# A bidirectional state-space layer with a soft mixture of experts: the order of the first transfers, of the constants and of the first silu

## The chip, the core and the metric

The kernel runs on one core of one Trainium2 chip. The metric is the device time of one launch in microseconds (us), from executions on the chip; the kernel before has a median of 5432.52 us over 3 runs (5432.14 to 5433.58). A core has five engines with a queue of instructions each: PE (matmul), DVE (vector), ACT (activation functions), POOL (a second vector engine) and SP, which here only issues DMAs. Each engine takes its instructions in the order of its queue; an instruction that waits for a semaphore holds everything behind it on that engine.

## What is computed

Sixteen sequences of 512 positions and 256 channels pass two layers, each with a residual and a layer norm. Cut to what matters:

```python
xr = x @ in_proj_w.T                      # 256 -> 2 x 512
xf, res = split(xr)
xf = silu(causal_conv(xf, conv_w, conv_b))          # 4 taps over positions
y  = ssm(xf, res, x_proj_w, dt_proj_w, dt_proj_b, A_log, D)
xb = silu(causal_conv(xf, conv_b_w, conv_b_b))
y += ssm(xb, res, ..., reverse=True)
x  = layernorm(x + y @ out_proj_w.T)
# ssm: A = -exp(A_log); dt, B, C = x @ x_proj_w.T; dt = softplus(dt @ dt_proj_w.T + b)
#      per state n of 16: a scan over the positions with decay exp(dt*A), input dt*u*B, output times C
#      y = (sum over states + u * D) * silu(res)

# second layer, a soft mixture of 16 experts with 64 slots each
x  = layernorm(x) * g + b
se = layernorm(slot_embeds) * slot_g + slot_b, times scale
logits = x @ se.T ; dispatch = softmax over positions ; combine = softmax over slots
slots = dispatch.T @ x ; eout = (gelu(slots @ Wg + bg) * (slots @ Wu + bu)) @ Wd + bd
x  = layernorm(x + combine @ eout)
```

## The kernel before

One sequence is handled at a time, channels on the 128 partitions and positions along the free axis. The 512 inner channels are four chunks (`ND`). For each sequence `scan_part` runs four times (forward and backward scan, two pairs of chunks); it walks over the 16 states in twos. For each pair of states and chunk POOL multiplies the input (`db`), ACT makes the decay (`h`, an exponential) and a factor (`th`, a tanh), DVE scans (`h`) and scales (`hg`), POOL multiplies by C (`hg` by `cs`), and PE adds the result up by transposing it into a PSUM bank (`acc`). The inputs `bs` and `cs` are broadcast rows of B and C, read back from a small DRAM buffer `bc`, which SP fills from `xd`.

Beside these scans the kernel does the rest in pieces. Generators yield after a group of matmuls; `beside_scan` takes one piece at a time from three lists: `prep` (the next chunks: `prep_forward`, `turn_back`, `prep_backward`, `prep_gate`, `prep_pair`), `front` (`moe_setup`, then `finish` of each sequence: output projection, layer norm, dispatch), and `back` (`experts` and `combine`, from sequence 3 on in every second sequence). The layer norms of these pieces go through `row_moments` (DVE: `bn_stats` and `bn_aggr` for each group of 128 rows), `factors` (POOL: the reciprocal root and the shift) and `scaled` (ACT).

Two things set the order of the instructions on each engine. The program text is the first. But a list scheduler stands behind it: it keeps the data dependences and moves instructions ahead of others where it expects their engine to be free. An instruction handed to `late` (`tc.keep_in_program_order`) keeps its place in the program's order relative to the others that are so marked; the unmarked ones may be put ahead of their place in the text. In `row_moments` of the kernel before nothing is marked, so the statistics of a group of rows can be put in as soon as these rows are there.

The beginning of the program is what most of the diff touches. In the kernel before it runs in this order:

- DVE clears `zeros` and `blank`; ACT issues four DMAs that clear `diag_dram` from `blank`.
- For the two directions in turn (the loop over `s, m`), SP loads the conv taps `cw`, `cb`, the three parts of `xT` (x_proj), `dtT`, `A`, `D`; ACT and DVE turn `A` into `-exp(A_log)` and half of it, and DVE fills the diagonal matrices `diagD`. Then SP loads `outT` (512 KB), which DVE halves.
- `prep_forward(0, 0, ND, fwd)` loads `x` of the first sequence with `load_x` (512 KB), PE transposes it (`ptx`), ACT copies it (`xT`); then for each chunk `project` loads 128 KB of `in_projT` (`w_pin`, two buffers), PE multiplies (`pin`), and `taps` forms the convolution: an Identity with scale and bias on ACT, then three multiply-adds on DVE. After the four chunks one silu covers all of them.
- `project_unit(0, 0, fwd)` multiplies by x_proj (`px`, four chunks accumulated in one bank), ACT evicts it (`xd`), SP writes `bc`, and ACT issues one DMA into `diag_dram`.
- `prep_pair(0, 0, 0, fwd)` makes the first two chunks of dt (`pz` on PE, softplus on ACT), `rr` (a scan on DVE) and `du` (POOL); then the first `scan_part` begins. `moe_setup`, whose tiles are the slot embeddings `se`, is listed first in `front`.

Each DMA of SP and ACT signals one of eight semaphores, taken in turn; a DMA that comes to a semaphore in use waits, in its queue, until the earlier DMA on it has landed.

Of the kernel before, what the change touches and what calls it, by code (L numbers as in the profile page):

```python
# [9 lines left out]
F32 = mybir.dt.float32  # L10
BF16 = mybir.dt.bfloat16
AF = mybir.ActivationFunctionType
# [5 lines left out]
P = 128  # L18
L = 512
NL = L // P  # L20
# [21 lines left out]

def row_moments(nc, pool, src, tag):

    k = src.shape[1]
    st = pool.tile([P, k, 6], F32, tag=f"{tag}_st", name=f"{tag}_st")
    mv = pool.tile([P, k, 2], F32, tag=f"{tag}_mv", name=f"{tag}_mv")
    for i in range(k):
        nc.vector.bn_stats(st[:, i, :], src[:, i, :])
        nc.vector.bn_aggr(mv[:, i, :], st[:, i, :])  # L50
    return mv


def seq_layers(tc, ident, neghalf, a, out):
# [22 lines left out]
    with ExitStack() as ctx:  # L77
# [33 lines left out]
        def load_x(b):  # L111
            xt = p1.tile([P, NL, DM], F32, tag="x", name=f"x_{b}")
            nc.sync.dma_start(xt, a["x"][b].rearrange("(c p) d -> p c d", p=P))
            return xt


        outT = const.tile([P, ND, DM], F32, name="outT")
        zeros = const.tile([P, L], BF16, name="zeros")
        nc.vector.memset(zeros, 0.0)
        blank = p2.tile([P, 4 * DM], F32, tag="W", name="blank", bufs=3)  # L120
        nc.vector.memset(blank, 0.0)
        for part in diag_dram.rearrange("r i l (p s) -> (r i) p l s", p=P):
            nc.scalar.dma_start(part, blank[:, : NL * (P + 1)].rearrange("p (l s) -> p l s", l=NL))

# [7 lines left out]

        side = []
        for s, m in (("f", ""), ("b", "_b")):
            w = {}
            w["cw"] = const.tile([P, ND, KW], F32, name=f"cw_{s}")
# [8 lines left out]

            nc.vector.tensor_scalar(w["xT"][:, :, XC:XW], w["xT"][:, :, XC:XW], 0.5, None, ALU.mult)
            w["dtT"] = const.tile([DTR + 1, DI], F32, name=f"dtT_{s}")
# [3 lines left out]
            nc.sync.dma_start(w["A"], a[f"A{m}_log"].rearrange("(c p) n -> p c n", p=P))  # L151
            nc.scalar.activation(w["A"], w["A"], AF.Exp)
            nc.vector.tensor_scalar(w["A"], w["A"], -1.0, None, ALU.mult)
            w["Ah"] = const.tile([P, ND, NS], F32, name=f"Ah_{s}")
            nc.vector.tensor_scalar(w["Ah"], w["A"], 0.5, None, ALU.mult)
            d = channels(a[f"D{m}"], f"D_{s}")
            w["diagD"] = const.tile([P, ND, P], F32, name=f"diagD_{s}")
            for c in range(ND):
                nc.vector.tensor_scalar(w["diagD"][:, c, :], ident, d[:, c : c + 1], None, ALU.mult)
            side.append(w)  # L160
        nc.sync.dma_start(outT, a["out_projT"].rearrange("(c p) o -> p c o", p=P))
        nc.vector.tensor_scalar(outT, outT, 0.5, None, ALU.mult)

        def late(ins):

            return tc.keep_in_program_order(ins)

# [15 lines left out]
        def project(xT, e, name, turned=False):  # L183

            wt = p2.tile([P, NM, P], F32, tag="inw", name=f"w_{name}")
            nc.sync.dma_start(wt, a["in_projT"].rearrange("(k p) e -> p k e", p=P)[:, :, e * P : (e + 1) * P])
            pp = bank(name)
            for lc in range(NL if turned else 0):
                s = slice(lc * P, (lc + 1) * P)
                for k in range(NM):  # L190
                    nc.tensor.matmul(pp[:, s], xT[:, k, s], wt[:, k, :], start=(k == 0), stop=(k == NM - 1))
            for k in range(0 if turned else NM):
                nc.tensor.matmul(pp, wt[:, k, :], xT[:, k, :], start=(k == 0), stop=(k == NM - 1))
            return pp

        def prep_forward(b, lo, hi, out):

            if lo == 0:
                xt = load_x(b)
                out["xT"] = p1.tile([P, NM, L], F32, tag="xT", name=f"xT_{b}")  # L200
# [11 lines left out]
            for c in range(lo, hi):  # L212
                yield GAP + 1
                pp = project(xT, c, f"pin_{b}_{c}")
                yield HOLD
                taps(xf[:, c, :], pp, side[0], c, xf[:, c, :])
            if hi == ND:
                yield 0
                late(nc.scalar.activation(xf, xf, AF.Silu))
                yield WAIT  # L220
                yield from project_unit(b, 0, out)
# [307 lines left out]
        def moe_setup():  # L529
# [4 lines left out]
            for t in (sg, sb):  # L534
                nc.vector.tensor_scalar(t, t, scale, None, ALU.mult)
            ses, src = [], a["slot_embeds"].rearrange("e s d -> (e s) d").rearrange("(h c p) d -> h p c d", p=P, c=4)
# [5 lines left out]
            yield 0  # L542
            stats = [factors(row_moments(nc, p2, se, "m1"), "m1") for se in ses]
            yield 0
# [44 lines left out]
        def finish(b, y):  # L589

            xt = load_x(b)
            for h in range(NL // 2):
# [25 lines left out]
                late(nc.vector.tensor_tensor(x2, x2, po, ALU.add))  # L618
            mv = row_moments(nc, p2, xt, "m1")
            yield WAIT  # L620
# [283 lines left out]
        def combine(b, kept=None):  # L904
# [20 lines left out]
            def moments(lo, hi):  # L925
                return row_moments(nc, p2, x1[:, lo:hi, :], f"c{hi - lo}"), f"c{hi - lo}"

# [140 lines left out]
```

## Time and profile before

| what | us |
|---|---|
| median of 3 runs | 5432.52 |
| the profiled execution, its own time | 5434.84 |
| the profiled execution, span of its instructions | 5432.9 |
| busy: POOL | 4732.3 |
| busy: DVE | 4552.0 |
| busy: PE | 4336.3 |
| busy: ACT | 4091.6 |
| POOL's first product (`du`) begins | 48.03 |
| first `db` of sequence 0, 1, 2, 3, 4, 5 begins | 50.7, 344.3, 643.3, 943.0, 1266.2, 1577.9 |
| first `db` of sequence 8, 9, 10 begins | 2548.5, 2857.8, 3184.6 |
| POOL idle within sequence 0, 1, 2 | 6.9, 5.8, 6.7 |
| POOL idle within sequence 8, 9 | 15.9, 30.6 |

The profile is of one execution; times inside it are counted from the start of its span, and its own time is 1.9 us longer than that span. A sequence here lasts from its first `db` on POOL to that of the next one. The last some 360 us, after the scans, are the tail: experts and combines of the last sequences, without POOL's products.

### The profile page before, as it was taken

What the parts mean: (1) busy time and instruction counts of PE and PEld (TensorE: products, weight loads), DVE (VectorE), ACT (ScalarE), POOL (GpSimd) and SP (SyncE); (2) the same over time, 40 slices, a digit from 0 to 9 for tenths busy, and PEclk for the clock granted to TensorE, in tenths of its full rate; (3) what the DMA queues carried; (4) which work ended last, traced back from release to release, by engine and by line L of the source; (5) the groups of instructions that cost most, each with busy time, mean ns of one, the idle gap of its engine ahead of it and who ended that gap; (6) DMA issues with size and microseconds to landing.
All of it is one profiled execution on the core that took longest, in us unless ns stands there. A gap on an engine that the chain in (4) does not pass through costs nothing. (4 is left out here: it accounts for less than half of the span.)

```text
span 5432.9 us, 73685 instructions
## 1 busy us (share of the span) xinstructions
PE 4336.3 (80%) x24145; PEld 3393.4 (62%) x24145; DVE 4552.0 (84%) x6276; ACT 4091.6 (75%) x6517; POOL 4732.3 (87%) x2537
## 2 busy tenths in 40 slices
PE   4656666898878977788788978889777887878889
PEld 3545555676667765677656766667656775667657
DVE  6888989889888898888988988988989889887722
ACT  6677777887788777887878887788778887777641
POOL 6999999999999899998999989998999989988600
PEclk7677878898889989899889988899888998989999
DMA  4333434575446754566446754467444774457435
GB/s 129 130 122 132 130 124 131 192 231 161 151 141 212 228 148 145 157 220 213 134 137 195 230 173 150 130 215 231 151 145 143 226 224 132 144 178 234 126 104 184
DMA packets 595237, 907.73 MB, mean 167 GB/s; under 512 B 78083, under 2 KB 384899, under 8 KB 594853
## 3 DMA queue, kind: packets, MB, share of 16 engines
q1 hardware_dynamic: 521156, 859.87, 49.9%
q10 hardware_dynamic: 73696, 43.14, 2.8%
q8 instruction: 192, 3.15, 0.2%
q14 instruction: 193, 1.57, 0.1%
HBM read 840.86 MB, written 62.01 MB: 166 GB/s over the span
## 5 line engine op out<-in xcount | busy, mean ns | idle before, releaser
L432 POOL TENSOR_TENSOR hg<-hg,cs 128x1024 f32<-128x1024 f32 x1024 | 2415.3, 2362 | 129.7 <-DVE hg L431 111.4
L403 POOL TENSOR_TENSOR db<-du,bs 128x1024 f32<-128x1024 f32 (+1 forms) x1024 | 2138.8, 2092 | 240.4 <-DVE h L426 93.5
L347 PE MATMUL acc<-ident,hg 128*128 128x128 f32 x8192 | 1191.7, 296 | 207.3 <-POOL hg L432 183.2
L431 DVE SCALAR_TENSOR_TENSOR hg<-th,h 128x512 f32<-128x512 f32 x1792 | 1186.2, 678 | 188.8 <-PE acc L347 110.4
L347 PEld LDWEIGHTS acc<-ident,hg 128*128 128x128 f32 x8192 | 1053.5, 155 | 399.4 <-POOL hg L432 251.0
L426 DVE TENSOR_TENSOR_SCAN h<-h,db 128x512 f32<-128x512 f32 x896 | 1071.3, 1218 | 97.5 <-ACT h L420 92.0
L428 DVE TENSOR_TENSOR_SCAN h<-h,db 128x512 f32<-128x512 f32 x896 | 1072.1, 1218 | 96.1 <-ACT h L420 92.9
L422 ACT ACTIVATE th<-rr,Ah_f 128x512 f32<-128x512 f32 x1024 | 724.5, 714 | 189.2 <-DVE hg L431 187.7
L422 ACT ACTIVATE th<-rr,Ah_b 128x512 f32<-128x512 f32 x1024 | 721.6, 712 | 166.1 <-DVE hg L431 151.3
L420 ACT ACTIVATE h<-dt,A_f 128x512 f32<-128x512 f32 x896 | 608.0, 681 | 115.2 <-DVE hg L431 112.1
L420 ACT ACTIVATE h<-dt,A_b 128x512 f32<-128x512 f32 x896 | 608.6, 681 | 105.0 <-DVE hg L431 102.9
L663 PE MATMUL pl<-x2T,seT 128*128 128x512 f32 x512 | 286.0, 687 | 73.6 <-DVE hg L431 36.2
L381 PE MATMUL hd<-dg,duT 128*128 128x128 f32 x2048 | 309.0, 300 | 35.3 <-ACT yt L603 15.2
L806 PEld LDWEIGHTS pg<-st,Wg 128*128 128x128 f32 x2048 | 245.4, 196 | 107.8 <-issue 85.4
L381 PEld LDWEIGHTS hd<-dg,duT 128*128 128x128 f32 x2048 | 286.1, 216 | 41.8 <-ACT yt L603 17.8
L938 PE MATMUL cpo<-ceo,ct 128*128 128x256 f32 x1024 | 266.3, 420 | 48.5 <-DVE rr L313 38.8
L782 PE MATMUL peo<-Wd,ht 128*128 128x256 f32 x1024 | 253.5, 403 | 48.2 <-DVE rr L313 30.5
L755 PE MATMUL pu<-st,Wu 128*128 128x128 f32 x2048 | 252.3, 282 | 44.6 <-DMA Wu<-in_Wu_dram 18.6
L755 PEld LDWEIGHTS pu<-st,Wu 128*128 128x128 f32 x2048 | 242.6, 196 | 55.8 <-DVE h L428 17.6
L938 PEld LDWEIGHTS cpo<-ceo,ct 128*128 128x128 f32 x1024 | 214.0, 213 | 99.6 <-DVE rr L313 44.0
L806 PE MATMUL pg<-st,Wg 128*128 128x128 f32 x2048 | 270.3, 287 | 5.6 <-DMA Wg<-in_Wg_dram 3.6
L860 PE MATMUL cl<-seT,cx 128*128 128x512 f32 x512 | 251.3, 631 | 29.1 <-ACT et L674 18.2
(151 smaller groups left out, 6621.3 us busy)
## 6 DMA issues: line engine op xcount, KB each, us to landing
cs<-bc SPq DMA_DIRECT2D x512, 512.0 KB, 4.0
bs<-bc SPq DMA_DIRECT2D x384, 512.0 KB, 5.0
Wg<-in_Wg_dram SPq DMA_DIRECT2D x128, 512.0 KB, 6.1
Wu<-in_Wu_dram SPq DMA_DIRECT2D x128, 512.0 KB, 5.7
Wd<-in_Wd_dram SPq DMA_DIRECT2D x128, 512.0 KB, 5.5
dg<-diag_dram SPq DMA_DIRECT2D x128, 256.0 KB, 4.4
bs<-bc SPq DMA_DIRECT2D x128, 256.0 KB, 3.6
x<-in_x_dram SPq DMA_DIRECT2D x32, 512.0 KB, 6.6
```

Source lines behind the costliest of these rows:

```text
L347: ins = nc.tensor.matmul(accs[c][:, s], hc[:, j, s], ident, is_transpose=True, start=False, stop=(last and j == 1 and lc == NL - 1),)
L381: ins = nc.tensor.matmul(h[:, s], v[c][3][:, s], dg[:, s], start=True, stop=True)
L403: nc.gpsimd.tensor_tensor(db[:, :k, :], du.unsqueeze(1).to_broadcast([P, k, L]), bs[:, :k, :], ALU.mult)
L420: nc.scalar.activation(hs[j][1], dt, AF.Exp, scale=w["A"][:, c, s])
L422: nc.scalar.activation(ths[j], rr, AF.Tanh, bias=LN_1E12 / 2, scale=w["Ah"][:, c, s])
L426: nc.vector.tensor_tensor_scan(h, dec, add, 0.0, ALU.mult, ALU.add)
L428: nc.vector.tensor_tensor_scan(h[:, ::-1], dec[:, ::-1], add[:, ::-1], 0.0, ALU.mult, ALU.add)
L431: nc.vector.scalar_tensor_tensor(hg[:, j, :], th, 1.0, h, ALU.add, ALU.mult)
L432: nc.gpsimd.tensor_tensor(hg, hg, cs, ALU.mult)
L755: nc.tensor.matmul(pu[:, fc * P : (fc + 1) * P], got["Wu", e][:, k, fc * P : (fc + 1) * P], st[:, k, :, j * SL : (j + 1) * SL], start=(k = ...
L806: nc.tensor.matmul(pg[:, fc * P : (fc + 1) * P], got["Wg", e][:, k, fc * P : (fc + 1) * P], st[:, k, :, j * SL : (j + 1) * SL], start=Fals ...
L938: nc.tensor.matmul(po[:, :DM], cts[sc // 4][:, sc % 4 * P : (sc % 4 + 1) * P], eos[sc // 4][:, sc % 4, :], start=(sc == 0), stop=(sc == NS ...
```

## The change

Four things are done.

- The first transfers are issued in another order: `x` of the first sequence and the first two `w_pin`, then the constants of the first projection (`projections` for the forward side), then the four DMAs from `blank`. All other constants are loaded in `constants()`, which is called after `prep_forward(0, ...)`. Their work on DVE (`diagD`, `xT`, `outT`) is marked `late`. The exponential of `A` and its two products form `decays`, called after `prep_pair(0, 0, 0, fwd)`.
- For the first sequence the silu is done chunk by chunk, each right after the chunk's taps; for the others it stays one operation on four chunks.
- `row_moments` takes `late` and marks the first `bn_stats` of every call, for all sequences.
- The products of the slot gains by `scale` in `moe_setup` are marked `late`.

The lines of the diff, without those that only hand `late` on:

```diff
@@ -40,13 +40,15 @@
 HOLD, WAIT, GAP = -1, -2, 8
 
 
-def row_moments(nc, pool, src, tag):
+def row_moments(nc, pool, src, tag, late):
 
     k = src.shape[1]
     st = pool.tile([P, k, 6], F32, tag=f"{tag}_st", name=f"{tag}_st")
     mv = pool.tile([P, k, 2], F32, tag=f"{tag}_mv", name=f"{tag}_mv")
     for i in range(k):
-        nc.vector.bn_stats(st[:, i, :], src[:, i, :])
+        ins = nc.vector.bn_stats(st[:, i, :], src[:, i, :])
+        if i == 0:
+            late(ins)
         nc.vector.bn_aggr(mv[:, i, :], st[:, i, :])
     return mv
 
@@ -113,14 +115,22 @@
             nc.sync.dma_start(xt, a["x"][b].rearrange("(c p) d -> p c d", p=P))
             return xt
 
-
-        outT = const.tile([P, ND, DM], F32, name="outT")
+        def load_in(e, name):
+            wt = p2.tile([P, NM, P], F32, tag="inw", name=f"w_{name}")
+            nc.sync.dma_start(wt, a["in_projT"].rearrange("(k p) e -> p k e", p=P)[:, :, e * P : (e + 1) * P])
+            return wt
+
+
+        first_x = [load_x(0)]
+        first_w = [load_in(c, f"pin_0_{c}") for c in range(2)]
+
+        def late(ins):
+
+            return tc.keep_in_program_order(ins)
+
+
         zeros = const.tile([P, L], BF16, name="zeros")
         nc.vector.memset(zeros, 0.0)
-        blank = p2.tile([P, 4 * DM], F32, tag="W", name="blank", bufs=3)
-        nc.vector.memset(blank, 0.0)
-        for part in diag_dram.rearrange("r i l (p s) -> (r i) p l s", p=P):
-            nc.scalar.dma_start(part, blank[:, : NL * (P + 1)].rearrange("p (l s) -> p l s", l=NL))
 
         unit = const.tile([XW, 1], F32, name="unit")
         nc.vector.tensor_copy(unit, ident[:XW, DTR : DTR + 1])
@@ -130,9 +140,9 @@
             nc.sync.dma_start(t, src.rearrange("(c p) -> p c", p=P))
             return t
 
-        side = []
-        for s, m in (("f", ""), ("b", "_b")):
-            w = {}
+        side = [{}, {}]
+
+        def projections(w, s, m):
             w["cw"] = const.tile([P, ND, KW], F32, name=f"cw_{s}")
             nc.sync.dma_start(w["cw"], a[f"conv{m}_w"].rearrange("(c p) o j -> p c (o j)", p=P))
             w["cb"] = channels(a[f"conv{m}_b"], f"cb_{s}")
@@ -143,27 +153,39 @@
             nc.sync.dma_start(w["xT"][:, :, XB : XB + NS], src[:, :, DTR : DTR + NS])
             nc.sync.dma_start(w["xT"][:, :, XC:XW], src[:, :, DTR + NS :])
 
-            nc.vector.tensor_scalar(w["xT"][:, :, XC:XW], w["xT"][:, :, XC:XW], 0.5, None, ALU.mult)
+            late(nc.vector.tensor_scalar(w["xT"][:, :, XC:XW], w["xT"][:, :, XC:XW], 0.5, None, ALU.mult))
+
+        def steps(w, s, m):
             w["dtT"] = const.tile([DTR + 1, DI], F32, name=f"dtT_{s}")
             nc.sync.dma_start(w["dtT"][:DTR, :], a[f"dt_proj{m}T"])
             nc.sync.dma_start(w["dtT"][DTR : DTR + 1, :], a[f"dt_proj{m}_b"].unsqueeze(0))
             w["A"] = const.tile([P, ND, NS], F32, name=f"A_{s}")
             nc.sync.dma_start(w["A"], a[f"A{m}_log"].rearrange("(c p) n -> p c n", p=P))
-            nc.scalar.activation(w["A"], w["A"], AF.Exp)
-            nc.vector.tensor_scalar(w["A"], w["A"], -1.0, None, ALU.mult)
-            w["Ah"] = const.tile([P, ND, NS], F32, name=f"Ah_{s}")
-            nc.vector.tensor_scalar(w["Ah"], w["A"], 0.5, None, ALU.mult)
             d = channels(a[f"D{m}"], f"D_{s}")
             w["diagD"] = const.tile([P, ND, P], F32, name=f"diagD_{s}")
             for c in range(ND):
-                nc.vector.tensor_scalar(w["diagD"][:, c, :], ident, d[:, c : c + 1], None, ALU.mult)
-            side.append(w)
-        nc.sync.dma_start(outT, a["out_projT"].rearrange("(c p) o -> p c o", p=P))
-        nc.vector.tensor_scalar(outT, outT, 0.5, None, ALU.mult)
-
-        def late(ins):
-
-            return tc.keep_in_program_order(ins)
+                late(nc.vector.tensor_scalar(w["diagD"][:, c, :], ident, d[:, c : c + 1], None, ALU.mult))
+
+        def decays(w, s):
+            late(nc.scalar.activation(w["A"], w["A"], AF.Exp))
+            late(nc.vector.tensor_scalar(w["A"], w["A"], -1.0, None, ALU.mult))
+            w["Ah"] = const.tile([P, ND, NS], F32, name=f"Ah_{s}")
+            nc.vector.tensor_scalar(w["Ah"], w["A"], 0.5, None, ALU.mult)
+
+        def constants():
+            steps(side[0], "f", "")
+            projections(side[1], "b", "_b")
+            steps(side[1], "b", "_b")
+            outT = const.tile([P, ND, DM], F32, name="outT")
+            nc.sync.dma_start(outT, a["out_projT"].rearrange("(c p) o -> p c o", p=P))
+            late(nc.vector.tensor_scalar(outT, outT, 0.5, None, ALU.mult))
+            return outT
+
+        projections(side[0], "f", "")
+        blank = p2.tile([P, 4 * DM], F32, tag="W", name="blank", bufs=3)
+        nc.vector.memset(blank, 0.0)
+        for part in diag_dram.rearrange("r i l (p s) -> (r i) p l s", p=P):
+            nc.scalar.dma_start(part, blank[:, : NL * (P + 1)].rearrange("p (l s) -> p l s", l=NL))
 
         def taps(dst, src, w, c, last):
 
@@ -182,8 +204,7 @@
 
         def project(xT, e, name, turned=False):
 
-            wt = p2.tile([P, NM, P], F32, tag="inw", name=f"w_{name}")
-            nc.sync.dma_start(wt, a["in_projT"].rearrange("(k p) e -> p k e", p=P)[:, :, e * P : (e + 1) * P])
+            wt = first_w.pop(0) if first_w else load_in(e, name)
             pp = bank(name)
             for lc in range(NL if turned else 0):
                 s = slice(lc * P, (lc + 1) * P)
@@ -196,7 +217,7 @@
         def prep_forward(b, lo, hi, out):
 
             if lo == 0:
-                xt = load_x(b)
+                xt = first_x.pop() if b == 0 else load_x(b)
                 out["xT"] = p1.tile([P, NM, L], F32, tag="xT", name=f"xT_{b}")
                 for k in range(NM):
                     yield 1
@@ -214,9 +235,12 @@
                 pp = project(xT, c, f"pin_{b}_{c}")
                 yield HOLD
                 taps(xf[:, c, :], pp, side[0], c, xf[:, c, :])
+                if b == 0:
+                    late(nc.scalar.activation(xf[:, c, :], xf[:, c, :], AF.Silu))
             if hi == ND:
                 yield 0
-                late(nc.scalar.activation(xf, xf, AF.Silu))
+                if b > 0:
+                    late(nc.scalar.activation(xf, xf, AF.Silu))
                 yield WAIT
                 yield from project_unit(b, 0, out)
 
@@ -532,7 +556,7 @@
             scale = const.tile([P, 1], F32, name="scale")
             nc.sync.dma_start(scale, a["scale"].unsqueeze(0).to_broadcast([P, 1]))
             for t in (sg, sb):
-                nc.vector.tensor_scalar(t, t, scale, None, ALU.mult)
+                late(nc.vector.tensor_scalar(t, t, scale, None, ALU.mult))
             ses, src = [], a["slot_embeds"].rearrange("e s d -> (e s) d").rearrange("(h c p) d -> h p c d", p=P, c=4)
             for h in range(NSC // 4):
                 se = p2.tile([P, 4 * DM], F32, tag="W", name=f"se_{h}", bufs=3)
@@ -540,7 +564,7 @@
                 nc.sync.dma_start(se, src[h])
                 ses.append(se)
             yield 0
-            stats = [factors(row_moments(nc, p2, se, "m1"), "m1") for se in ses]
+            stats = [factors(row_moments(nc, p2, se, "m1", late), "m1") for se in ses]
             yield 0
             for se, (rs, sh) in zip(ses, stats):
                 scaled(se, se, sh, rs)
@@ -960,9 +984,13 @@
 
         FINISH, COMBINE, PAIR = 32, 14, 4
         fwd = {}
-        for gen in (prep_forward(0, 0, ND, fwd), prep_pair(0, 0, 0, fwd)):
-            prep.add(1, gen)
+        prep.add(1, prep_forward(0, 0, ND, fwd))
         prep.drain()
+        outT = constants()
+        prep.add(1, prep_pair(0, 0, 0, fwd))
+        prep.drain()
+        for w, s in zip(side, "fb"):
+            decays(w, s)
         front.add(8, moe_setup())
         for b in range(nb):
             bwd, nxt, accs = {}, {}, {}
```

More of the change, by code (lines that the diff above doesn't have):

```diff
@@ L618, in finish @@
                 late(nc.vector.tensor_tensor(x2, x2, po, ALU.add))
-            mv = row_moments(nc, p2, xt, "m1")
+            mv = row_moments(nc, p2, xt, "m1", late)
             yield WAIT
@@ L925, in moments @@
             def moments(lo, hi):
-                return row_moments(nc, p2, x1[:, lo:hi, :], f"c{hi - lo}"), f"c{hi - lo}"
+                return row_moments(nc, p2, x1[:, lo:hi, :], f"c{hi - lo}", late), f"c{hi - lo}"
             def put(lo, hi, rs, sh):
```

## The prediction

> **What bounds the kernel now.** I read the page's busy shares and slices first, then the waits of the opening 110 us, then the timelines engine by engine, there and around the stalls of the loop. In a timeline line the columns are start, length, engine, line, operation, tiles and, in brackets, the idle time before it and what ended it.
>
> ```profile
> PE 4336.3 (80%) x24145; PEld 3393.4 (62%) x24145; DVE 4552.0 (84%) x6276; ACT 4091.6 (75%) x6517; POOL 4732.3 (87%) x2537
> ...
> POOL 6999999999999899998999989998999989988600
> ```
>
> The reader is to see that POOL is 90% busy or more in nearly all slices, and empty only at the start and in the last two slices (the tail, which PE carries). So the loop costs POOL's work plus POOL's idle time: an edit pays where POOL starts sooner or waits less.
>
> ```profile
> PE ptx L205 <- DMA x<-in_x_dram: 19.1, 1, 19.1
> ACT L219 <- DVE xf L177: 3.7, 1, 3.7
> PE px L258 <- ACT xf L219: 7.8, 1, 7.8
> POOL du L315 <- ACT dt L296: 46.0, 1, 46.0
> ```
>
> POOL's first product waits 46.0 us. The chain to it, from the timelines of the five engines:
>
> ```profile
> 13.95 0.47 SPq L113 DMA_DIRECT2D x<-in_x_dram  x1
> 17.06 1.19 SPq L540 DMA_DIRECT2D se<-in_slot_embeds_dram  x2
> 19.13 1.94 PE L205 MATMUL ptx<-ident,x 128*128 128x128 f32 x8 [19.13 <-DMA x<-in_x_dram]
> 30.10 0.78 ACT L171 ACTIVATE xf<-pin,cb_f,cw_f 128x512 f32<-128x512 f32 x1 [0.94 <-PE pin L193]
> 34.58 1.28 ACT L219 ACT_TABLE_LOAD   x1 [3.70 <-DVE xf L177]
> 35.87 1.91 ACT L219 ACTIVATE xf<-xf 128x2048 f32<-128x2048 f32 x1
> 37.83 6.21 PE L258 MATMUL px<-xf,xpT_f 128*80 128x512 f32 x8 [7.78 <-ACT xf L219]
> 44.08 0.68 ACT L265 ACTIVATE xd<-px,unit 80x512 f32<-80x512 f32 x1 [6.30 <-PE px L258]
> 48.03 2.50 POOL L315 TENSOR_TENSOR du<-dt,xf 128x512 f32<-128x512 f32 x2 [45.98 <-ACT dt L296]
> ```
>
> x is issued only at 13.95, behind 21 constants; the silu waits for all four chunks, and all eight passes of px wait for the silu. In the loop one stall returns in each even sequence from 4 to 14. This is the one of sequence 8, on POOL, ACT and DVE:
>
> ```profile
> 2739.57 0.22 POOL L575 TENSOR_SCALAR c_rs<-c_mv 128x4 f32<-128x4 f32 x1
> 2748.53 2.34 POOL L403 TENSOR_TENSOR db<-du,bs 128x1024 f32<-128x1024 f32 x1 [2.39 <-DVE h L426]
> 2741.55 1.58 ACT L583 ACTIVATE cx<-cx,c_sh,c_rs 128x256 f32<-128x256 f32 x3 [4.16 <-POOL c_sh L578]
> 2744.48 0.68 ACT L420 ACTIVATE h<-dt,A_f 128x512 f32<-128x512 f32 x1
> 2745.26 1.23 DVE L426 TENSOR_TENSOR_SCAN h<-h,db 128x512 f32<-128x512 f32 x1 [5.64 <-ACT h L420]
> ```
>
> ACT stands for the row factors c_sh, which POOL makes behind a product; the exponential h is queued behind that wait, DVE's scan waits for h, and POOL for the scan.
>
> **What the Trainium skill says.** "ScalarE: Activation LUTs", What ACT_TABLE_LOAD costs: 1283 ns of load whatever the set; the trace agrees (1.28 us). The same page, Table sets: cheap functions such as identity are in every set, so an Identity after a Silu needs no new load; the trace agrees, since the Identity at 44.08 follows the silu at 35.87 with none between. "DMA: Bandwidth & Descriptors", Anatomy of one DMA: about 2 us fixed (stated for the other issue path), and a semaphore wait holds the issuing sequencer; here w_pin of 128 KB lands 2.3 us after its issue. "TensorE: Matmul & The Clock Gate", The HAM clock gate: an idle array restarts at half rate; here pin's passes took 592 to 1219 ns, so I keep the slow ones.
>
> **The change part by part.** The changed program's instruction order gives each queue; durations are the rows of before.
>
> *x first.* x is issued at about 0.7. outT, as large, needed 3.9 us (12.34 to 16.27, where DVE scales it), x itself 5.2, so x lands at 4.7 to 5.9. ACT is not ready then: its four blank DMAs and a table load stand ahead of the first xT copy, the fourth DMA waits for the first one's landing, and before this block ended at 7.82. I take the copies at 7.9 to 8.9 and the first Identity 2.0 later, as before (21.69 to 23.71): 10.9.
>
> *Chunk by chunk.* On ACT the order is now Identity 0, silu 0, Identity 1, and so on, so the chunks no longer overlap: one costs 0.78 (Identity) + 2.1 (three taps on DVE of 0.65 to 0.74) + 0.6 (a quarter of the 1.91 silu and its start) + 0.1 = 3.6 us. Chunk 0 with its table load ends at 10.9 + 3.6 + 1.3 = 15.8, chunk 1 at 19.4.
>
> *A new wait.* Row statistics of the slot embeddings stand on DVE inside chunk 2, behind its first tap, waiting for the first se tile, with five taps queued behind. On SP that tile is number 30, behind the constants; the DMAs use eight semaphores in turn, so number 6 waits for x and w_pin 2 (number 22) goes out near 15, landing by 17.3. The se tile then goes out near 19 and lands at 23 to 25 (4 to 6 us for 512 KB). Chunk 2 would reach that wait at 20.8: I take 2.2 us of stall (0 to 4) and 0.9 of the statistics. So chunk 2 ends at 26.1, chunk 3 at 29.7. Three quarters of px lie beside this; the last two passes cost about 2: xd at 31.6, not 44.08. Gain 12.5 (11 to 15).
>
> *Moved constants.* diagD (8 of 0.28), xpT_b and the scaling of outT (0.69), some 3 us on DVE, now lie between the last tap and the softplus, where DVE idled 13.48: nothing. The two exponentials of A (0.26 each) and their DVE products go behind both rr scans (2.33), so the first h starts 0.9 later; its scan waits for db until 53.04 against 51.3, so it is covered, and 0.9 if not. DMAs of later weights move ahead of bc on SP but are issued by about 29. Of the slot statistics 2.6 us fall into the scan near 88 us on the old clock, beside one product of POOL (2.35) and the factors there (93.28 to 97.3): nothing.
>
> *Pinned statistics in the loop.* The first bn_stats of each group keeps its place, and the list scheduler reorders around it. In even sequences 4 to 14 POOL makes c_rs to c_sh before one db (2.36) instead of after it, and ACT puts h ahead of two copies (about 1.0). c_mv is ready by 2736.0, before POOL would ask at 2737.2. h comes up to 3.7 earlier, DVE's 5.64 shrinks by that, and POOL's 2.39 goes: 6 x 2.4 = 14.4. Late next is the db at 2760.72 (2.89 idle behind DVE's cnm), whose chain runs through the same DVE queue and moves along. In odd sequences 5 to 13 the two Gelu calls now stand together, sparing one load of the four in this block, where POOL idles 3.96; one exponential (0.62) moves in behind c_sh: 5 x (1.28 - 0.62) = 3.3 gained.
>
> ```profile
> 2899.46 1.28 ACT L823 ACT_TABLE_LOAD   x1
> 2901.37 1.28 ACT L235 ACT_TABLE_LOAD   x1
> 2904.59 1.28 ACT L826 ACT_TABLE_LOAD   x1
> ```
>
> Against that, the x statistics bunch: three bn_stats with their sums (0.35 + 0.09 each) stand before a scan where there were two. In odd sequences POOL waited 0.96 for that scan, so I charge 0.5 in seven of them: 3.5 lost. In even ones POOL does not idle within 130 us: nothing.
>
> *Sum.* 12.5 + 14.4 + 3.3 - 3.5 = 26.7. The profiled execution took 5434.84 (span 5432.9), so 5408.1; the median shown lies 2.3 below that execution: 5406.
>
> **The rivals.** (1) The loop's gain is swallowed by its next wait, and only the start counts: 5432.5 - 12.5 = 5420. For it: the 2.89 behind cnm stands 12 us later. Against: that wait is made of DVE work which moves too. (2) The start also gives little: the se tile at 25 or later, w_pin 3 held up beside outT, a late blank; xd near 38 and no loop gain: 5426. For it: 21 DMAs stand between x and w_pin 2. Against: w_pin 2 was issued at 23.7 before. In that case the change hardly does what it says. (3) Slower: the bunched x statistics. In even sequences one scan moves behind three bn_stats, their sums and an hg step (0.6), at most 1.9 us. If POOL waits for all of it in 15 sequences, 28 us are lost against 12.5: 5449. It decides from 12.5 / 15 = 0.83 us a sequence on. For it: DVE has no idle time there (2624 to 2645). Against: POOL has none either, so it works from a lead.
>
> **How the numbers follow.** The forecast has 0.55 (its own range 5393 to 5415), rival 1 0.22 (5416 to 5425), rival 2 0.13, rival 3 0.10. Low end: no se stall (15) and up to 3.7 kept in each even sequence: 5432.5 - 15 - 22, less the rest, 5390 at the furthest I believe. High end: rival 2 with some of rival 3's loss, 5432. 0.2% is 10.9 us, about what a measurement of this kernel can tell from no change. Faster: all of the forecast and two thirds of rival 1, 0.70; same: the rest of it and rival 2, 0.20; slower: 0.10.
>
> **What would show it.** POOL's first product near 35.5; PE's first transposes near 5.3; a DVE wait for an se tile inside the taps of 1 to 4 us; four Identity and silu pairs on ACT, 3.6 us apart; five table loads fewer; in sequence 8 c_rs right behind one db and POOL's 2.39 gone; sequences 0 to 2 unchanged in length (293.7, 299.0, 299.7 between their first db). Even sequences longer than 330 us, or POOL's start later than 42, would make it wrong.

## The result, and the profile after

The changed kernel takes 5411.04 us in the median of 6 runs (5406.55 to 5412.12), the kernel before in the same rounds 5432.33 (5424.75 to 5436.25, 6 runs): a ratio of 0.9961 with a 95% interval of 0.9948 to 0.9974, so 14 to 28 us less. One execution of the whole study, of the kernel with the mark in `finish` below, ran at a lower granted clock (0.784 against 0.885 to 0.892 in the others) and took 5587.52; it is left out of all comparisons. The profiled execution took 5411.23 (span 5409.4), 23.5 less in span than that of the kernel before.

The page's busy line and slices first:

```profile
PE 4331.1 (80%) x24144; PEld 3390.0 (63%) x24145; DVE 4559.7 (84%) x6276; ACT 4087.2 (76%) x6515; POOL 4732.1 (87%) x2537
...
POOL 6999999999999899998999989998999989988600
```

POOL has the same work to 0.2 us. What was gained is time in which POOL waited, at the start and in the loop, and 1.8 us behind the loop. The waits of the opening 110 us (engine, line and releaser: us in total, times, longest):

```profile
POOL du L339 <- ACT dt L320: 36.2, 1, 36.2
...
ACT L230 <- DMA diag_dram<-blank: 8.2, 1, 8.2
...
PE ptx L226 <- DMA x<-in_x_dram: 4.9, 1, 4.9
```

POOL's first wait is 9.8 shorter (46.0 before), PE's for x 14.2 shorter (19.1 before). So a third of what x gained is lost on the way. The timelines of the engines show where:

```profile
4.88 1.94 PE L226 MATMUL ptx<-ident,x 128*128 128x128 f32 x8 [4.88 <-DMA x<-in_x_dram]
10.08 5.86 PE L214 MATMUL pin<-xT,w_pin 128*128 128x512 f32 x8 [3.26 <-ACT xT L230]
...
2.22 5.90 ACTq L188 DMA_DIRECT2D diag_dram<-blank  x4
8.15 1.28 ACT L230 ACT_TABLE_LOAD   x1 [8.15 <-DMA diag_dram<-blank]
9.45 1.07 ACT L230 COPY xT<-ptx 128x512 f32<-128x512 f32 x2
13.90 0.78 ACT L193 ACTIVATE xf<-pin,cb_f,cw_f 128x512 f32<-128x512 f32 x1 [3.38 <-PE pin L214]
...
22.14 0.63 ACT L239 ACTIVATE xf<-xf 128x512 f32<-128x512 f32 x1 [2.44 <-DVE xf L199]
...
27.81 0.63 ACT L239 ACTIVATE xf<-xf 128x512 f32<-128x512 f32 x1 [4.38 <-DVE xf L199]
...
34.26 0.68 ACT L289 ACTIVATE xd<-px,unit 80x512 f32<-80x512 f32 x1 [2.08 <-PE px L282]
...
25.59 0.43 DVE L49 BATCH_NORM_STATS2 m_st<-se 128x6 f32<-128x256 f32 x1 [1.37 <-DMA se<-in_slot_embeds_dram]
```

In the kernel before, the four blank transfers and the same eight passes of pin took less:

```profile
2.22 4.29 ACTq L123 DMA_DIRECT2D diag_dram<-blank  x4
...
20.90 4.49 PE L193 MATMUL pin<-xT,w_pin 128*128 128x512 f32 x8
```

PE has transposed x at 6.8, but ACT copies it only at 9.45: its queue holds four blank transfers for 5.90 us, behind which the table load starts at 8.15 (6.54 before). PE, idle until then, does pin slowly, and the first Identity comes at 13.90. From silu 1 (22.14) to silu 2 (27.81) a chunk takes 5.67 instead of 3.74: the slot statistics stand between its taps, 1.37 of it waiting for the se tile.

In the loop this is sequence 8, on POOL, ACT and DVE:

```profile
2727.66 0.23 POOL L599 TENSOR_SCALAR c_rs<-c_mv 128x4 f32<-128x4 f32 x1
...
2736.56 2.34 POOL L427 TENSOR_TENSOR db<-du,bs 128x1024 f32<-128x1024 f32 x1
...
2746.81 1.27 POOL L427 TENSOR_TENSOR db<-du,bs 128x512 f32<-128x512 f32 x1 [0.97 <-POOL hg L456]
...
2729.65 1.59 ACT L607 ACTIVATE cx<-cx,c_sh,c_rs 128x256 f32<-128x256 f32 x3 [2.08 <-POOL c_sh L602]
2731.14 0.67 ACT L444 ACTIVATE h<-dt,A_f 128x512 f32<-128x512 f32 x1
...
2731.91 1.23 DVE L450 TENSOR_TENSOR_SCAN h<-h,db 128x512 f32<-128x512 f32 x1 [0.87 <-ACT h L444]
```

ACT waits 2.08 for c_sh instead of 4.16, DVE's scan 0.87 instead of 5.64, and the db that waited 2.39 (2736.56) follows its predecessor at once. The 512-wide db behind it waits 0.97. Before, it waited 2.89 for DVE's cnm, which itself had stood 1.20 for PE's product (cl); in the changed kernel this wait of DVE is gone:

```profile
2760.72 1.27 POOL L403 TENSOR_TENSOR db<-du,bs 128x512 f32<-128x512 f32 x1 [2.89 <-DVE cnm L870]
```

### The profile page after: what moved, and what is told of

It is laid out like the page before. It is cut to its first block, busy times and chain, and to the rows that moved or that the text cites. A ratio compares the mean times of both kernels' runs of the same rounds, so it can differ in the third digit from the quotient of the medians.

```text
span 5409.4 us, 73721 instructions
## 1 busy us (share of the span) xinstructions
PE 4331.1 (80%) x24144; PEld 3390.0 (63%) x24145; DVE 4559.7 (84%) x6276; ACT 4087.2 (76%) x6515; POOL 4732.1 (87%) x2537
## 5 line engine op out<-in xcount | busy, mean ns | idle before, releaser
L371 PE MATMUL acc<-ident,hg 128*128 128x128 f32 x8192 | 1179.3, 295 | 203.3 <-POOL hg L456 181.6
L687 PE MATMUL pl<-x2T,seT 128*128 128x512 f32 x512 | 299.1, 715 | 78.7 <-DVE hg L455 37.4
L962 PE MATMUL cpo<-ceo,ct 128*128 128x256 f32 x1024 | 254.8, 407 | 46.9 <-DVE rr L337 39.9
L806 PEld LDWEIGHTS peo<-Wd,ht 128*128 128x128 f32 x1024 | 205.3, 206 | 97.7 <-DVE rr L337 41.2
```

Source lines behind the costliest of these rows:

```text
L371: ins = nc.tensor.matmul(accs[c][:, s], hc[:, j, s], ident, is_transpose=True, start=False, stop=(last and j == 1 and lc == NL - 1),)
L806: nc.tensor.matmul(po[:, j * DM : (j + 1) * DM], ht[:, fc, :], got["Wd", e0 + j][:, fc, :], start=(fc == 0), stop=(fc == NF - 1),)
```

## The experiments

Sequences are measured in one way for all runs, in POOL's timeline: from a sequence's first forward `du` to that of the next. (Ahead of the prediction a sequence went from first `db` to first `db`; here a wait between the first du and the first db lies inside sequence 0, 12.13 us in *start again* and 5.60 in *start, third*.) "Marks" or "pins" are the `late` on the first `bn_stats` of a group. All in us, from one profiled execution each:

| kernel | first db | sequences 0 to 2 | 3 | even, 4 to 14 | odd, 5 to 13 |
|---|---|---|---|---|---|
| before | 50.7 | 883.2 | 323.2 | 1853.6 | 1649.7 |
| changed | 40.7 | 885.3 | 326.4 | 1834.4 | 1651.8 |
| changed, again | 40.2 | 884.1 | 322.3 | 1834.0 | 1649.6 |
| start alone | 41.5 | 885.0 | 323.3 | 1853.6 | 1657.4 |
| all pins alone | 51.4 | 882.4 | 325.0 | 1834.0 | 1646.7 |
| pin of combine alone | 52.1 | 882.3 | 323.1 | 1842.1 | 1647.0 |
| pin of finish alone | 51.6 | 883.4 | 326.5 | 1860.3 | 1647.8 |
| decays early | 42.2 | 883.2 | 321.4 | 1838.0 | 1648.8 |
| silu whole | 45.8 | 883.0 | 321.8 | 1835.5 | 1647.5 |
| slot statistics pinned | 39.3 | 886.7 | 326.8 | 1834.4 | 1648.8 |
| start again | 45.9 | 898.5 | 326.0 | 1836.2 | 1647.5 |
| start, third | 38.8 | 890.6 | 326.5 | 1837.4 | 1649.6 |

**Is it the start, the loop, or both?** First the change without the marks on the layer norms of the loop:

```diff
-            mv = row_moments(nc, p2, xt, "m1", late)
+            mv = row_moments(nc, p2, xt, "m1")
...
-                return row_moments(nc, p2, x1[:, lo:hi, :], f"c{hi - lo}", late), f"c{hi - lo}"
+                return row_moments(nc, p2, x1[:, lo:hi, :], f"c{hi - lo}"), f"c{hi - lo}"
```

> The start of the change without the pinned statistics in the loop (the first bn_stats of finish and combine free again; every loop then has the instruction order of the kernel before). Theory A (two sums: the start's 9.9 us less 1.7 lost in sequence 0, and the loop's own 15): 5424, between 5420 and 5428, and sequences 3 to 14 as long as before. Rival B (all of it is the start; the loop's differences come from the earlier start): 5411, and the even sequences are shorter by 3 to 4 us although their order is unchanged.

Then the kernel before with the marks in all three calls of `row_moments` and nothing else:

```diff
-        nc.vector.bn_stats(st[:, i, :], src[:, i, :])
+        ins = nc.vector.bn_stats(st[:, i, :], src[:, i, :])
+        if late and i == 0:
+            late(ins)
```

> The pinned statistics alone, on the start of before (the loop then has the changed kernel's order). Theory A: 5417, between 5413 and 5421, first db at 50.7 as before, even sequences 4 to 14 shorter by about 3.5 us, sequence 3 longer by 3. Rival B: 5432, all sequences as before.

The start alone has 5429.98 (21 runs), ratio 0.9985 (0.9978 to 0.9992); the marks alone 5420.35 (6 runs), ratio 0.9971 (0.9959 to 0.9982); before in these rounds 5437.19 (35 runs), some 5 more than in the first rounds, so the ratios are to be compared and not the times (5429.98 lies above the 5420 to 5428 that were expected of the start alone). The start is worth 0.15%, some 8 us, the marks 0.29%, some 16. Together 0.15% and 0.29% make 0.44%, beside 0.39% measured for the change: both parts count, and they add up. The table says where: the start alone leaves the even sequences at 1853.6 to the tenth, the marks alone bring them to 1834.0, as in the change. (The odd ones of the start alone are 7.7 longer with every instruction in the order of before; so much can a column move from one execution to the next.)

**Which mark?** The marks alone, once in `combine` only and once in `finish` only:

```diff
-                return row_moments(nc, p2, x1[:, lo:hi, :], f"c{hi - lo}"), f"c{hi - lo}"
+                return row_moments(nc, p2, x1[:, lo:hi, :], f"c{hi - lo}", late), f"c{hi - lo}"
```

> Only combine's statistics pinned, on the start of before. Theory A says that the even sequences gain because the row factors of combine come before one product on POOL, and that bunching the x statistics costs: so this alone gains more than all pins together, even sequences shorter by about 4, sequence 3 unchanged, odd ones shorter by 0.7 or more since 15 table loads go instead of 5: 5402, between 5395 and 5412. Rival C (the even sequences gain from the reordered x statistics): 5430, even sequences as before.

```diff
-            mv = row_moments(nc, p2, xt, "m1")
+            mv = row_moments(nc, p2, xt, "m1", late)
```

> Only the statistics of finish (x) pinned, on the start of before. Theory A: slower, 5438, between 5433 and 5445: sequence 3 longer by 3 us, the odd ones by about 1 to 2, the even ones as before. Rival C: 5412, even sequences shorter by 3 to 4.

The mark in combine: 5420.68 (6 runs), ratio 0.9971 (0.9959 to 0.9982); in finish: 5439.30 (12 runs), 1.0004 (0.9995 to 1.0012). By these medians combine's mark has the whole gain of all marks (5420.35), though not the 5402 that was expected of it, and finish's has none. The columns seem to say something else: 11.5 in the even sequences from combine alone, 19.6 from all marks, and 6.7 lost with finish alone. But they are one execution each, and that of combine (5426.25) was the slowest of its six. POOL's waits in the traces are plainer. The db that waited 2.39 before, in sequence 8, with combine's mark alone and then with finish's alone:

```profile
2741.97 2.36 POOL L405 TENSOR_TENSOR db<-du,bs 128x1024 f32<-128x1024 f32 x1
```

```profile
2754.40 2.34 POOL L405 TENSOR_TENSOR db<-du,bs 128x1024 f32<-128x1024 f32 x1 [2.38 <-DVE h L428]
```

This wait is there in all six even sequences of before, of the start alone and of finish alone, and in none of combine alone, of all marks and of the change: combine's mark removes it. Finish's mark brings a wait of its own. Before and in the changed kernel, earlier in sequence 8:

```profile
2650.82 2.36 POOL L403 TENSOR_TENSOR db<-du,bs 128x1024 f32<-128x1024 f32 x1
```

```profile
2640.72 2.37 POOL L427 TENSOR_TENSOR db<-du,bs 128x1024 f32<-128x1024 f32 x1 [0.75 <-DVE h L452]
```

These 0.75 to 0.77 us stand in every even sequence from 4 to 14 of the nine runs with that mark, and in none of the three without it: 4.6 us in six sequences. Whether the mark gives anything for it beside combine's was not shown: with the same order of instructions, the even sequences of combine alone lie between 304.6 and 308.7 us.

The first of these kernels also speaks against a gain from the table loads: it has 15 fewer in the loop (327 for 342), ACT is busy 17 us less (4074.5 for 4091.6), and the odd sequences, where they are spared, are 2.7 shorter in all; with the mark in finish, which spares none, they are 1.9 shorter. By the prediction's 0.66 for each, 9.9 were to be expected; a few us would not be seen.

**The products of A.** In the changed kernel's timelines of DVE and POOL the products of A stand out, which the prediction's sum has at their old length:

```profile
40.71 6.95 POOL L427 TENSOR_TENSOR db<-du,bs 128x1024 f32<-128x1024 f32 x3
...
41.01 2.10 DVE L171 TENSOR_SCALAR A_f<-A_f 128x64 f32<-128x64 f32 x1 [0.35 <-ACT A_f L170]
43.14 2.27 DVE L173 TENSOR_SCALAR Ah_f<-A_f 128x64 f32<-128x64 f32 x1
45.33 2.38 DVE L171 TENSOR_SCALAR A_b<-A_b 128x64 f32<-128x64 f32 x1
...
47.86 2.34 DVE L450 TENSOR_TENSOR_SCAN h<-h,db 128x512 f32<-128x512 f32 x2
```

Before, each of them took 0.19 to 0.20, as this one:

```profile
9.70 0.19 DVE L153 TENSOR_SCALAR A_f<-A_f 128x64 f32<-128x64 f32 x1
```

POOL's three db of 2.32 end at 43.0, 45.3 and 47.7; the three products end at 43.1, 45.4 and 47.7. They were put ahead of POOL's work again:

```diff
         outT = constants()
-        prep.add(1, prep_pair(0, 0, 0, fwd))
-        prep.drain()
         for w, s in zip(side, "fb"):
             decays(w, s)
+        prep.add(1, prep_pair(0, 0, 0, fwd))
+        prep.drain()
```

> The changed kernel with one move: the exponentials and the four small DVE products of A (128x64 each) stand ahead of the first softplus instead of behind the first two rr scans. Theory A: these products took 2.10 to 2.38 us each in the changed kernel only because POOL's db products were running beside them (each ended as a db product ended; with POOL idle they took 0.19 to 0.20 before). With POOL idle they take 0.2 us each again, DVE's first scan h starts near 43.5 instead of 47.9, ACT's waits of 2.02 and 1.67 for A_f and Ah_f go, and POOL's idle time in sequence 0 falls by 1.7; the extra stretch on ACT ahead of the softplus (a table load of 1.28 and 0.5 of exponentials, part of it beside pz) delays POOL's first product by 0.6 to 1.8. Net gain at sequence 1: 0 to 1.1 us; the whole time, within noise of the changed kernel (5411). Theory B: the products are slow because of their data (freshly landed constants) or their shape: they take 2 us again and push the rr scans and POOL's start back by 6 us.

DVE's timeline in that run:

```profile
37.65 0.20 DVE L171 TENSOR_SCALAR A_f<-A_f 128x64 f32<-128x64 f32 x1 [4.10 <-ACT A_f L170]
37.88 0.20 DVE L173 TENSOR_SCALAR Ah_f<-A_f 128x64 f32<-128x64 f32 x1
37.99 0.19 DVE L171 TENSOR_SCALAR A_b<-A_b 128x64 f32<-128x64 f32 x1
...
44.60 1.23 DVE L450 TENSOR_TENSOR_SCAN h<-h,db 128x512 f32<-128x512 f32 x1 [2.57 <-ACT h L444]
```

With the same data and shape they take 0.20 when POOL is idle: theory B falls. Sequences 0 to 2 are back at 883.2, the length of before, from 885.3 and 884.1 in the two executions of the change; but the first db is 1.5 later (42.21), since the exponentials now hold the softplus. How much of these 2.1 is the products' is not clean: the kernel with the silu whole (below) has two of them at 2.27 and 2.23, and still 883.0. One run took 5409.58; the change was not run in those rounds, and the kernel before took 5439.72 there, 7 more than in the first, so no difference can be told.

**The silu in chunks and the wait for se.** The first silu whole again, and all slot statistics marked instead of the first of four:

```diff
-                if b == 0:
-                    late(nc.scalar.activation(xf[:, c, :], xf[:, c, :], AF.Silu))
             if hi == ND:
                 yield 0
-                if b > 0:
-                    late(nc.scalar.activation(xf, xf, AF.Silu))
+                late(nc.scalar.activation(xf, xf, AF.Silu))
```

> The changed kernel with the first silu whole again, behind all four chunks. Theory A: the chunks' Identities and taps overlap again, but w_pin 3 and 4 still land only near 18.7 and 22.2, so the last tap ends near 27 to 28, the silu (1.28 load, 1.91) near 31, and all eight passes of px (6.2 us) stand behind it: xd near 37, 2.5 to 3.5 later than the 34.26 of the changed kernel; so of the start's gain the silu in chunks is worth 3 and the earlier x the other 7. Theory B: the serial chain of chunks (Identity, taps, silu, 3.74 each) costs as much as it hides: xd within 1 us of 34.26 or earlier.

```diff
-        if i == 0:
+        if every or i == 0:
             late(ins)
...
-            stats = [factors(row_moments(nc, p2, se, "m1", late), "m1") for se in ses]
+            stats = [factors(row_moments(nc, p2, se, "m1", late, True), "m1") for se in ses]
```

> The changed kernel with all four row statistics of each slot-embedding tile pinned, not the first alone; they then stand behind the first scans instead of between the taps of chunk 2. Theory A: the wait of 1.37 for the se tile and its 1.0 of statistics go out of the taps, chunk 2's silu ends near 26.0 instead of 28.4 and xd comes at 31.9 to 32.6 instead of 34.26; POOL starts near 36 instead of 38.21. Theory B: the chunk is held by w_pin 4 (which lands near 22.2) and by PE, so xd moves by less than 0.7.

With the silu whole, xd comes at 39.36, 5.1 later (2.5 to 3.5 expected; the last Identity waits for pin until 26.69, and px and the silu follow it undivided). Of the 9.8 at xd the chunks are thus worth 5.1 and the earlier x 4.7, in these two executions: beside the repeat of the change (xd at 33.35) it is 6.0, and a part is pin, whose last four passes took 3.75 here and 1.95 in the change. With the slot statistics out of the taps, xd comes at 32.31, 2.0 earlier (1.0 than in the repeat), POOL starts at 36.27, and the chunk takes 3.74 instead of 5.67: the wait was on the path, as the prediction had it. But sequences 0 to 2 are 1.4 longer than in the change (2.6 than in the repeat), so most of it is not kept. One run each, 5413.52 and 5413.26, in the same rounds as the one before: no time can be told from these.

**Can the start be had better?** Two kernels with a start redone; the core of the first:

```diff
-        first_w = [load_in(c, f"pin_0_{c}") for c in range(2)]
+        first_w = []
+        room = p1.tile([P, ND, L], F32, tag="res", name="w_first")
+        for c in range(ND):
+            wt = room[:, c, : NM * P].rearrange("p (k e) -> p k e", k=NM)
+            nc.sync.dma_start(wt, a["in_projT"].rearrange("(k p) e -> p k e", p=P)[:, :, c * P : (c + 1) * P])
+            first_w.append(wt)
...
-            nc.scalar.dma_start(part, blank[:, : NL * (P + 1)].rearrange("p (l s) -> p l s", l=NL))
+            nc.gpsimd.dma_start(part, blank[:, : NL * (P + 1)].rearrange("p (l s) -> p l s", l=NL))
...
-                if b == 0:
-                    late(nc.scalar.activation(xf[:, c, :], xf[:, c, :], AF.Silu))
+                if b == 0 and c > 0:
+                    late(nc.scalar.activation(xf[:, c - 1, :], xf[:, c - 1, :], AF.Silu))
```

> The changed kernel with its start redone and one pin limited: all four first w_pin tiles loaded ahead of the constants (into a tile that is free then); the blank transfers on POOL's queue instead of ACT's; each chunk's silu behind the next chunk's Identity, so that taps follow taps; all slot statistics pinned; the products of A ahead of the first softplus; the pin in the statistics of x only from sequence 3's finish on, so not in sequence 3. Theory A: copies of xT near 6 instead of 9.45, first Identity near 10.8, taps of 2.3 us each without a gap, xd near 23.5 instead of 34.26, POOL's first product near 27.5 to 29 and first db near 30 to 31, 10 us ahead of the changed kernel; sequence 3 back at 323 instead of 326.4 (3 us); the rest as in the changed kernel: 5411 - 13 = 5398 against 5432 of before, 0.6%. Theory B: what the start gains is lost again in the first sequences, as POOL's early work then waits for weights and DMAs: the first db is 10 us earlier but the start of sequence 2 less than 3 us, and the time stays at 5408 or above.

The queue of SP and POOL's timeline in it:

```profile
37.81 0.38 SPq L427 DMA_DIRECT2D dg<-diag_dram  x1
...
38.82 0.38 SPq L423 DMA_DIRECT2D bs<-bc  x1
...
31.24 2.49 POOL L346 TENSOR_TENSOR du<-dt,xf 128x512 f32<-128x512 f32 x2 [24.96 <-ACT dt L327]
45.86 6.96 POOL L434 TENSOR_TENSOR db<-du,bs 128x1024 f32<-128x1024 f32 x3 [12.13 <-DMA bs<-bc]
```

POOL begins 7.0 earlier, and then waits 12.13 for bs. `dg` are diagonal matrices that SP reads back from `diag_dram` for PE. On SP the scheduler had put dg ahead of bs, and dg waits for ACT's element-wise write of the diagonal, issued at 26.28: 4 KB, which 11.5 us later had just landed. So bs was issued only at 38.82, and the first db came 7.0 later. Theory B holds for the time, but not in its detail: the first db is 5.2 later than in the change, where it expected it 10 earlier. The median is 5416.65 (5 runs), ratio 0.9954 (0.9941 to 0.9968), no better than the change. The second one marks that dg, loads A with the first weights and keeps the blank transfers on ACT, two at a time between the chunks:

```diff
+                    if b == r == p == n - 2 == 0:
+                        late(ins)
...
+                    for part in blanks[2 * (c - 1) : 2 * c]:
+                        late(nc.scalar.dma_start(part, blank[:, : NL * (P + 1)].rearrange("p (l s) -> p l s", l=NL)))
```

> The changed kernel with its start redone a second time: the two biases and scales of the convolution, both A and all four first w_pin tiles right behind x; the exponentials and products of A before the first Identity, where ACT waits for PE; the blank transfers on ACT's queue but two at a time between Identity and silu; each chunk's silu behind the next chunk's Identity; all slot statistics pinned; the first dg transfer held behind the first two pairs of bs and cs on SP. Theory A: first Identity at 9.5 to 11, taps without gaps, xd at 22 to 24, POOL's first product at 25 to 27 and, unlike in the run before, no wait of 12 us for bs behind dg (at most 2), so first db at 28 to 30 instead of 40.71, first h scan behind it without the 2 us products of A; 11 to 14 us less than the changed kernel at the start of sequence 1 and to the end: 5397 to 5402, ratio to before 0.993 to 0.994. Theory B: a transfer holds it again (dg on SP for some 11 us behind the element-wise write of the diagonal, or bs), the gain at the start of sequence 1 is under 5 us, and the time is within 3 us of the changed kernel's in the same rounds.

ACT, SP and POOL:

```profile
20.98 0.63 ACT L255 ACTIVATE xf<-xf 128x512 f32<-128x512 f32 x1 [4.37 <-issue]
...
28.20 0.33 SPq L312 DMA_DIRECT2D bc<-xd  x1
...
32.78 0.34 SPq L434 DMA_DIRECT2D bs<-bc  x1
...
38.83 6.95 POOL L447 TENSOR_TENSOR db<-du,bs 128x1024 f32<-128x1024 f32 x3 [5.60 <-DMA bs<-bc]
```

The first Identity is at 9.78 as expected, but ACT stands 4.37 before a silu, behind the third and fourth blank transfers, and from bc to bs it takes 4.6 us where the change needed 1.6 (34.97 to 36.56). bc also took longer to land, 5.0 us after its issue for 1.9 in the change, and bs 5.9 for 3.8. The first db is 1.9 earlier than in the change, not 11 to 13. The median is 5407.02 (5 runs), ratio 0.9949 (0.9935 to 0.9962); the changed kernel in the same rounds 5411.44 (5 runs), 0.9954 (0.9941 to 0.9966). The intervals overlap: no version was shown to beat the change. Whether bc is slow because weights were issued just ahead of it was not tried.

> The changed kernel itself again, in the same rounds as the redone start. Its time is to be within 0.2% of its first measurement (5411). Sequence 3 tells two theories apart. Theory A: the 3 us by which sequence 3 was longer than before (326.4 against 323.2) came with the granted clock of TensorE in that execution: px there took 6.62 us instead of 5.01; if it takes about 5 here, sequence 3 is 321 to 323.5 long. Theory B: the pinned statistics of x cost it: sequence 3 is 326 again while px takes 5.

The changed kernel again: sequence 3 is 322.3 here. PE's timeline in the first execution, then in this one:

```profile
981.27 6.62 PE L282 MATMUL px<-xb,xpT_b 128*80 128x512 f32 x8 [3.84 <-ACT xb L259]
```

```profile
979.21 5.00 PE L282 MATMUL px<-xb,xpT_b 128*80 128x512 f32 x8 [3.76 <-ACT xb L259]
```

The same eight passes behind the same wait; the granted clock from 979 to 991 us was 0.72 and 0.88. This speaks for theory A, that the 4 us between the two are not the change's; so does the start again, whose sequence 3 has no mark in `finish` and still took 326.0, with px at 6.64. The Trainium skill, "TensorE: Matmul & The Clock Gate", Part 1, says that the window which sets the clock is free-running, so that a ramp differs from run to run; this pair agrees.

## Why the prediction was right

5406 was predicted and 5411.04 measured; the sum of 26.7 lies within the 14 to 28 of the interval, and both of its parts are real. That the total came so near is in part luck: in the profiled execution the start and sequences 0 to 3 gave about 8 us less than said, the even sequences 4.8 more. By the medians of the parts the start is worth some 8 us for 12.5, the marks some 16 for 14.2. By its own steps, in the profiled execution (predicted, measured; the last column from the table above):

| step | predicted | measured |
|---|---|---|
| start, to the first du | 12.5 | 9.8 (again: 10.7) |
| sequences 0 to 2 | 0 | -2.1 (again: -0.9) |
| sequence 3 | 0 | -3.2 (again: +0.9) |
| even, 4 to 14 | 14.4 | 19.2 (again: 19.6) |
| odd, 5 to 13 | 3.3 - 3.5 | -2.1 (again: +0.1) |
| sequence 15 and the tail | 0 | 1.8 (again: -3.7) |
| sum | 26.7 | 23.5 (again: 26.7) |

- *x first.* PE's transposes came at 4.88 (5.3 said). The step "I take the copies at 7.9 to 8.9 and the first Identity 2.0 later" was mis-sized. It took the block of blank transfers and table load as it was before; but the four transfers took 5.90 on ACT's queue for 4.29, so the copies came at 9.45. And PE, idle for 3.26 before pin, took 5.86 for what had taken 4.49. The Identity came at 13.90, 3.0 late; xd 2.7 late.
- *Chunk by chunk.* 3.74 a round for 3.6: right.
- *The new wait* for se: 1.37 for 2.2, within its bounds, and on the path: with the slot statistics out of the taps xd came 2.0 earlier.
- *Moved constants.* The step "its scan waits for db until 53.04 against 51.3, so it is covered, and 0.9 if not" failed. It took the durations of before (0.2) into a place where POOL's products run. DVE's first scan ended behind three products of 2.1 to 2.4, and POOL idled 3.79 before its first hg (1.25 in the repeat), where it had not waited before. Sequences 0 to 2, which were to stay as long as they were, became 2.1 and 0.9 longer; a part of that may have other causes (see above).
- *Even sequences.* The mechanism is right: c_rs ahead of the db, h ahead of the copies, POOL's 2.39 gone. The size was low: 3.2 a sequence, not 2.4, because the next wait (2.89 behind cnm) did not merely move along but shrank to 0.97. Against that, the bunched statistics of x, which were put at nothing in even sequences, brought 0.75 to 0.77 in each.
- *Odd sequences.* Nothing in sum, as said, but not by the two terms that were said to cancel. Five table loads are gone, as said (337 for 342). The spared load shortened DVE's wait for h and gave POOL nothing. POOL before, in sequence 9; then ACT, DVE and POOL in the changed kernel:

```profile
2911.93 2.37 POOL L403 TENSOR_TENSOR db<-du,bs 128x1024 f32<-128x1024 f32 x1 [3.96 <-DVE h L426]
```

```profile
2890.09 1.28 ACT L847 ACT_TABLE_LOAD   x1
2891.39 0.60 ACT L847 ACTIVATE ht<-pg 128x512 f32<-128x512 f32 x1
2891.88 0.59 ACT L850 ACTIVATE ht<-pg 128x512 f32<-128x512 f32 x1
...
2894.58 1.23 DVE L450 TENSOR_TENSOR_SCAN h<-h,db 128x512 f32<-128x512 f32 x1 [3.42 <-ACT h L444]
...
2887.02 2.36 POOL L427 TENSOR_TENSOR db<-du,bs 128x1024 f32<-128x1024 f32 x1 [1.51 <-DVE h L450]
...
2897.92 2.38 POOL L427 TENSOR_TENSOR db<-du,bs 128x1024 f32<-128x1024 f32 x1 [1.60 <-DVE h L450]
...
2908.19 1.28 POOL L427 TENSOR_TENSOR db<-du,bs 128x512 f32<-128x512 f32 x1 [1.54 <-DVE h L450]
```

The two Gelu calls share a load, and DVE waits 3.42 instead of 6.17; but POOL's one wait of 3.96 has become three of 1.51, 1.60 and 1.54, and the sequence is as long as it was (329.3 for 329.5). And the mark in finish alone, which bunches the statistics, did not lengthen the odd sequences (1647.8); its 0.76 is in the even ones.

Rival 1 (only the start counts) fell with the marks alone, rival 2 with xd at 34.26 and the gain of the loop, rival 3 with the mark in finish, the nearest to it, at 1.0004: at most 1.0012, some 6.5 us, is far from its 28. Its wait is there, but at 0.76 in each even sequence it is a fraction of what it feared.

## What to carry to other kernels

Price the path into a start on each engine's queue: what was gained at x was lost again behind four transfers on ACT's queue, and two redone starts met the next transfer (dg, bs) instead. A duration holds only for the neighbours it was measured beside, so a step that is moved next to another engine's work is to be priced there. A load or a wait that is spared counts only if the engine that sets the end waits less in sum: compare its idle time over the whole sequence, not at the one place.

## What the runs showed of the hardware

- A DVE product by a scalar of 128x64 takes 0.19 to 0.20 us with POOL idle and up to 2.38 beside POOL's products, until these end; in the repeat of the changed kernel every second one slipped through (0.20, 2.31, 0.18, 2.23), the first of them while POOL stood idle before its first db. The Trainium skill, "SBUF — State Buffer", Who interferes with whom, has the mechanism: such products can enter a mode that takes the port pair shared with GpSimd (POOL), and who comes second waits for the whole instruction. The ends agree to 0.1 us; that it is the port was not separated from other causes.
- The element-wise write of 4 KB of diagonal (ACT's DMA from xd) released the read behind it after 11.5 us in one run, and after 10.7 (27.49 to 38.14) and 11.8 (34.97 to 46.81) in two others.
- The same code took 326.4 and 322.3 us in sequence 3, and the longer one goes with a lower granted clock of TensorE (0.72 for 0.88 during px): px took 5.0 to 5.1 or 6.6 in all runs here, and no sequence 3 with 6.6 was shorter than 325.0; of those with 5.0 to 5.1 one was as long (326.8, slot statistics pinned), where POOL waits 1.42 and 3.51 for DVE, over 100 us behind px; why stays open.
